# A two-layer equivariant graph network on one core: products in one PSUM tile, node sums turned once and repeated by transfers, layer 1's transfers in fewer shares

## The chip, the cores and the metric

The kernel runs on one core of a Trainium2 chip. The metric is the device time of one execution in microseconds (us), as the median of several executions. The engines are named as in the profile: PE (TensorE, matmuls), PEld (its weight load), DVE (VectorE), ACT (ScalarE), POOL (GpSimd) and SP (SyncE, which here issues transfers).

## The reference

There are N = 6250 nodes with 160 features each (64 scalars, and 32 vectors of 3) and E = 100000 edges, sorted by their target `dst`. Two layers run one after the other, each on the layer-normalised and rectified features, and each is added to `x`.

```
# layer 0
m0, m1 = tp(h[dst], edge_attr_4, wm...)        # one message per edge
msgs   = merge(m0 + lin(h0, lm0), m1 + lin(h1, lm1))
agg    = segment_sum(msgs, src)                # row = src: the messages are NOT sorted by this
a0, a1 = split(agg); x0, x1 = split(h)         # 64 scalars, 32 x 3 vector parts
u0 = einsum('eu,ev,uvw->ew',  x0, a0, wu000) + isq3 * einsum('euk,evk,uvw->ew', x1, a1, wu110)
u1 = einsum('eu,evk,uvw->ewk', x0, a1, wu011) + einsum('euk,ev,uvw->ewk', x1, a0, wu101)
x  = x + h + merge(u0 + lin(x0, lu0), u1 + lin(x1, lu1))
# layer 1
messages = products(h[src], edge_attr_4, W...) * sigmoid(edge_attr_16 @ W_rad.T + b_rad)
agg      = segment_sum(messages, dst)          # sorted by this
x        = x + lin(h + agg, L_s, L_v)
```

The costly part is the product `u`: for each node, two feature vectors `x` and `a` are multiplied in all pairs and the pairs are contracted with weight tensors `wu...`.

## The kernel before

The program has three stages that follow one another.

**scatter()** (L445 to 648) makes layer 0's messages, in 782 tiles of 128 edges. Since they are not sorted by the node that sums them, each tile works out the rank of its edges among those of the same block of nodes (PE L567 and L568), forms the messages on PE (L569), and POOL sends the tile to its places in a DRAM table `msgs` by one indirect transfer (L587). Behind it, the messages of each block of nodes lie together.

**update()** (L650 to 1030) sums the messages per node and forms the product `u`. It goes in 13 groups: twelve of 500 nodes and a last one of 250. For one group:

- `fetch(k)` (L710) loads the messages of four blocks ("a quad") from `msgs` into `urec`, by four transfers that SP issues. Three quads are fetched ahead.
- `sums(g, a)` (L723 to 784) is a generator whose steps are strewn into the group before. `ones` (L728) makes one-hot matrices `uhot` of which message belongs to which node (on ACT, L746 and L749; for group 0 on DVE). PE multiplies them with `urec` (L761, 32 matmuls per quad), which gives the sums with nodes on the partitions. ACT copies them into `ag` (L767, L769), with the 64 scalar columns written twice and each of the three sets of 32 vector columns four times. PE then turns each of the four 128-wide slices (L782), and ACT copies it to `a[:, j]` (L778): `a[:, 0]` is the scalars repeated twice over the 128 partitions, and `a[:, 1..3]` are the vector parts repeated four times.
- `Group.first` (L853) is one of the 32 steps that `plan` lists: 16 of kind "x", 8 of kind "v", 8 of kind "y". Each takes a tile `y` of two PSUM banks from the pool `py`, which has two such tiles. PE fills it by matmuls (L860 for a "y" step, L879 for the others, which merely repeat rows of `x` or `v` over the partitions), and DVE multiplies it with `a` (L882), in a "y" step twice, with `a[:, 1:]` and with `x1k` (L864, two instructions). POOL adds the halves of "y" products (L867), multiplies and adds those of "v" steps (L849, L887).
- `second` (L895) contracts the products with weights on PE into `out0` and `out1`, some steps later (`later`: 2, 8 and 4 steps).
- `back()` (L902 to 974), strewn into the group after, turns the result, adds it to `x`, normalises it and stores what layer 1 gathers, the table `T1` (L972, L973).

The order on PE, DVE, ACT and POOL is written by hand (the loop at L997 to 1025 walks through all steps of all groups); the order of SP's transfers is left to the scheduler. Instructions wait for each other by semaphores, which the framework puts in by following who last read or wrote a tile.

**windows()** (L1059 to 1280) is layer 1, in 131 sets of 6 tiles of 128 edges. POOL gathers the rows of `T1` (L1087, 782 indirect transfers, two sets ahead), PE computes the gates (L1106), ACT and DVE form the messages, and PE adds them into windows of 32 nodes with one-hots `whot` (L1124, L1243). SP writes each window to a DRAM table (L1253), and loads the edge attributes in pieces of `CH` = 2 sets (`piece`, L1042).

A path for other inputs, `general()`, is not run here.

Of the kernel before, what the change touches and what calls it, by code (L numbers as in the profile page):

```python
# [23 lines left out]
P = 128  # L24
# [18 lines left out]
CH = 2  # L43
# [13 lines left out]
def gnn_kernel(ctx: ExitStack, tc: tile.TileContext, a: dict, out: bass.AP):  # L57
# [47 lines left out]
    def edge_attr(pool):  # L105
        t = pool.tile([P, ET, 4], F32, name="attr")
        nc.sync.dma_start(t, a["attr4"])
        return t
# [541 lines left out]
    def update():  # L650
# [3 lines left out]
        with ExitStack() as s:  # L654
# [8 lines left out]
            py = s.enter_context(tc.tile_pool(name="py", bufs=2, space=PSUM))  # L663
# [41 lines left out]
            last = []  # L705
# [4 lines left out]
            def fetch(k):  # L710

                if k >= len(quads):
                    return
                g, q = quads[k]
                b0, nq = groups[g][0] // BW + q, min(4, groups[g][1] // BW - q)
                got[g, q] = recs.tile([P, 4, 4, F + 1], F32, name="urec")
                for b in range(nq):
                    with tc.issue_after(last[-1]) if last else nullcontext():
                        at = nc.sync.value_load(start_i[0:1, b0 + b:b0 + b + 1], min_val=0, max_val=E)
                    last.append(nc.sync.dma_start(got[g, q][:, b], msgs[bass.ds(at, CAP), :]  # L720
                                                  .rearrange("(p i) f -> p i f", i=4)).ins)

            def sums(g, a):  # L723

                r0, n = groups[g]
                qs = [(q, min(4, n // BW - q)) for q in range(0, n // BW, 4)]
                hots, ags = [], []

                def ones(q, nq):


                    rl = two.tile([P, 4, 4], F32, name="rl")
                    nc.scalar.activation(rl[:, :nq], got[g, q][:, :nq, :, F], AF.Copy, scale=-1.0,
                                         bias=float(r0 + q * BW))
                    hot = two.tile([P, 4, 4, 32], F32, name="uhot")
                    hots.append(hot)
                    if g == 0:
                        nc.vector.tensor_tensor(hot[:, :nq].rearrange("p b i n -> p i b n"),
                                                node[:, None, :nq].to_broadcast([P, 4, nq, 32]),
                                                rl[:, :nq].rearrange("p b i -> p i b")[:, :, :, None]  # L740
                                                .to_broadcast([P, 4, nq, 32]), op=OP.add)
                        nc.vector.tensor_single_scalar(hot[:, :nq], hot[:, :nq], 0.0, op=OP.is_equal)
                        return
                    for b in range(nq):
                        for i in range(4):
                            nc.scalar.activation(hot[:, b, i], node[:, b], AF.Square, bias=rl[:, b, i:i + 1])  # L746
                        if b % 2:
                            yield
                    nc.scalar.activation(hot[:, :nq], hot[:, :nq], AF.Relu, scale=-1.0, bias=1.0)  # L749
                    yield  # L750

                yield from ones(*qs[0])
                yield
                for j, (q, nq) in enumerate(qs):
                    if g == 0 and j + 1 < len(qs):
                        yield from ones(*qs[j + 1])
                    p = pt.tile([P, 4 * P], F32, name="ptr")
                    rec, hot = got.pop((g, q)), hots.pop(0)
                    for i in range(4):
                        for b in range(nq):  # L760
                            nc.tensor.matmul(p[32 * b:32 * b + 32, :F], hot[:, b, i], rec[:, b, i, 0:F],  # L761
                                             start=i == 0, stop=i == 3, tile_position=(0, 32 * b))
                    fetch(quads.index((g, q)) + 3)
                    yield
                    w = 32 * nq
                    ag = pool.tile([P, 4, P], F32, name="ag", bufs=5)
                    nc.scalar.copy(ag[:w, 0].rearrange("p (i f) -> p i f", i=2),  # L767
                                   p[:w, None, 0:M0].to_broadcast([w, 2, M0]))
                    nc.scalar.copy(ag[:w, 1:].rearrange("p k (i f) -> p k i f", i=4),  # L769
                                   p[:w, M0:F].rearrange("p (k f) -> p k f", k=3)[:, :, None]  # L770
                                   .to_broadcast([w, 3, 4, M1]))
                    ags.append(ag)
                    if g and j + 1 < len(qs):
                        yield from ones(*qs[j + 1])
                    yield
                for j in range(5):
                    if j:
                        nc.scalar.copy(a[:, j - 1, :n], p[:, :n])  # L778
                    if j < 4:
                        p = pt.tile([P, 4 * P], F32, name="ptr")  # L780
                        for ag, (q, nq) in zip(ags, qs):
                            nc.tensor.matmul(p[:, q * BW:(q + nq) * BW], ag[:32 * nq, j],  # L782
                                             quad[:32 * nq, :nq].rearrange("p b n -> p (b n)"), start=True, stop=True)
                        yield
# [19 lines left out]
            halves = (slice(0, M0), slice(M0, P))  # L804

# [9 lines left out]
            class Group:  # L815
# [37 lines left out]
                def first(self, kind, c):  # L853
# [3 lines left out]
                    y = py.tile([P, 2, 4 * P], F32, name="y")  # L857
# [119 lines left out]
            with tc.manual_schedule(engines={eng.PE, eng.DVE, eng.Activation, eng.Pool}):  # L977
# [13 lines left out]

                for k in range(3):
                    fetch(k)
                gs = {0: Group(0)}
# [39 lines left out]
    def early(pool):  # L1034
# [7 lines left out]
        def piece(k, pool):  # L1042
            t0 = k * CH * GB
            nt = min(CH * GB, ET - t0)
            if nt > 0:
                nq = -(-nt // GB)
                bufs = 3 if pool is e["pool"] else 6
                t = e["attr"][k] = pool.tile([P, CH * GB, 4], F32, name="wattr", bufs=bufs)
                nc.sync.dma_start(t[:, :nt], a["attr4"][:, t0:t0 + nt])
                t = e["blk"][k] = pool.tile([GB * 16 + 1, CH, P], F32, name="wblk", bufs=bufs)  # L1050
                for r in (slice(0, K), slice(K, K + 1)):
                    nc.sync.dma_start(t[r, :nq], a["attr16"][r, k * CH:k * CH + nq])

        e["piece"] = piece
        for k in range(3):
# [3 lines left out]
    def windows(e):  # L1059
# [3 lines left out]
        with ExitStack() as s:  # L1063
# [7 lines left out]
            fin = s.enter_context(tc.tile_pool(name="wf", bufs=3))  # L1071

# [38 lines left out]
            def messages(u, ps):  # L1111
# [12 lines left out]
                nc.vector.tensor_tensor(hot[:, :nt], lane[:, None, :WN].to_broadcast([P, nt, WN]),  # L1124
# [109 lines left out]
            def add(u):  # L1234
                t0, nt = sets[u]
                hot, ms = ready.pop(u)
                for i in range(nt):
# [7 lines left out]
                    if t0 + i == end and (w % 4 == 3 or w + 1 == NW):  # L1245
                        o = pool.tile([P, F], F32, name="wo", bufs=3)
                        nc.scalar.copy(o[:j + WN], state["acc"][:j + WN])  # L1247
                        for x in range(w - w % 4, w + 1):
# [4 lines left out]
                            wrote.append(nc.sync.dma_start(agg[x % 2][bass.ds(row, WN), :],  # L1253
# [4 lines left out]
            with tc.manual_schedule(engines={eng.PE, eng.DVE, eng.Activation, eng.Pool}):  # L1258
                for u in range(2):
                    gather(u)  # L1260
                for k in range(3, 7):
                    e["piece"](k, pre)
# [27 lines left out]
    def parts(const, keep):  # L1290
# [119 lines left out]
        def edges(layer):  # L1410
# [5 lines left out]
            with ExitStack() as s:  # L1416
# [29 lines left out]
                def gate(t0, nt):  # L1446
                    q, half = t0 // GB, t0 % GB // NT
                    k = q // CH
                    if k not in blocks:
                        nq = min(CH, a["attr16"].shape[1] - k * CH)  # L1450
                        blocks[k] = ep.tile([GB * 16 + 1, CH, P], F32, name="blk")
                        nc.sync.dma_start(blocks[k][:, :nq], a["attr16"][:, k * CH:k * CH + nq])
# [264 lines left out]
def _layout(i):  # L1717
# [21 lines left out]

    L0 = {k[7:]: v for k, v in i.items() if k.startswith("L0_gnn_")}  # L1740
# [9 lines left out]
    o["attr4"] = padded(i["edge_attr_4"], nt * P, 0).reshape(nt, P, 4).transpose(1, 0, 2)  # L1750
# [6 lines left out]
    o["attr16"] = t16  # L1757
# [47 lines left out]
```

## Time and profile before

| what | us |
|---|---|
| median of three executions | 3076.58 (3076.5 to 3080.14) |
| the profiled execution | 3756.65 |
| its span in the profile | 3754.5 |
| scatter, from the start to the last scatter's issue | 1367.8 |
| update(), groups 0 to 11, from the first product | 874 |
| update(), last group | about 45 |
| windows() | about 1425 |

The profiled execution took 680 us more than the median. Times within it are compared with each other; a step that is worked out from its rows is put against its own time first. Its mean granted PE clock is 0.744 of full speed: near 1 in `update()`, 0.6 to 0.7 in the two other stages. A row of the profile gives the line of the code, the engine, the operation, the tile written and the tiles read with their partitions and elements, the number of instructions, their busy time and the mean of one in ns, and then the engine's idle time just before them with the instruction that ended it.

### The profile page before, as it was taken

How to read it: one execution, taken by the hardware profiler on the slowest of the kernel's cores; microseconds unless marked ns; L12 is line 12 of the kernel's file. 1: busy time of each engine (PE TensorE's matmuls, PEld its weight loads, DVE VectorE, ACT ScalarE, POOL GpSimd, SP SyncE). 2: the span in 40 equal slices, each digit the busy share in tenths (PEclk: the TensorE clock that was granted, in tenths of full speed). 3: DMA queues.
4: the chain of work that ended last, by engine and by line, in shares of the span. 5: the costliest groups of instructions: out<-in, count | busy, mean ns of one | idle time of the engine just before them, and what ended most of it. 6: DMA issues, size and time to landing. Idle time of an engine off the chain costs nothing.

```text
span 3754.5 us, 47926 instructions
## 1 busy us (share of the span) xinstructions
PE 2422.0 (65%) x12112; PEld 1279.0 (34%) x12112; DVE 2213.9 (59%) x4577; ACT 1546.3 (41%) x5127; POOL 2216.2 (59%) x1864
## 2 busy tenths in 40 slices
PE   5655565655544439999999998455555566655655
PEld 3433344443333323333333332132322233332323
DVE  6564555555544437777877775455655556555554
ACT  4445454554444424544453441333433333333433
POOL 4565565655666637777777775655555555555552
PEclk8677766776766659999999999566766666566666
DMA  6555555654544456665655542445444444445442
GB/s 176 157 167 153 167 162 153 180 162 144 148 126 136 136 173 187 180 183 159 178 178 175 165 119 70 130 131 147 133 136 133 137 139 139 131 135 147 133 132 73
DMA packets 346121, 554.56 MB, mean 148 GB/s; under 512 B 63954, under 2 KB 245168, under 8 KB 339947
## 3 DMA queue, kind: packets, MB, share of 16 engines
q1 hardware_dynamic: 230840, 291.12, 28.3%
q0 software_dynamic: 87584, 218.31, 20.0%
q10 hardware_dynamic: 27411, 41.99, 3.4%
q8 instruction: 99, 1.62, 0.2%
q14 instruction: 187, 1.53, 0.1%
HBM read 418.16 MB, written 133.04 MB: 147 GB/s over the span
## 4 chain that ended last, share of the span: by engine, by line
PE 29%; another core or an unknown queue 21%; DVE 17%; ACT 14%; issue 11%; DMA 4%; SPq 2%; POOL 1%; ACTq 1%; DVEq 0%; POOLq 0%
PE out L895 5%; ACT wm L1118 4%; ACT junk L580 4%; DVE pr L864 4%; PE pmsg L569 3%; PE y L879 2%; PE wbank L1243 2%; PE wgate L1106 2%; PE y L860 2%; PE wbank L1175 2%; DVE wtb L1132 2%; PE rank L568 2%; PE ptr L782 2%; DVE wm L1142 1%
## 5 line engine op out<-in xcount | busy, mean ns | idle before, releaser
L587 POOL DMA_INDIRECT msgs<-rec,pos_i x782 | 780.7, 998 | 572.4 <-issue 216.8
L1087 POOL DMA_INDIRECT wgot<-T,src_i x782 | 739.1, 945 | 635.7 <-issue 427.8
L567 PE MATMUL rank<-seen,every 128*128 128x256 f16 x782 | 264.7, 339 | 500.8 <-ACT junk L580 359.1
L580 ACT ACTIVATE junk<-rank,off 128x256 bf16<-128x256 f32 x782 | 373.2, 477 | 388.1 <-remote 280.4
L569 PE MATMUL pmsg<-tw,d 120*128 120x160 f32 x1564 | 470.5, 392 | 54.1 <-issue 38.7
L1106 PE MATMUL wgate<-wrad,wblk 97*128 97x480 f32 x522 | 376.3, 854 | 175.2 <-issue 127.8
L882 DVE TENSOR_TENSOR pr<-y,a 128x1000 f32<-128x1000 f32 (+1 forms) x312 | 352.4, 1151 | 129.5 <-PE y L879 128.8
L867 POOL TENSOR_TENSOR pr<-pr 128x1500 f32<-128x1500 f32 (+1 forms) x104 | 338.1, 3251 | 148.5 <-DVE pr L864 148.4
L1124 DVE TENSOR_TENSOR whot<-lane,wbank 128x192 f32<-128x192 f32 x131 | 45.8, 349 | 616.1 <-ACT wbank L1232 559.0
L1243 PE MATMUL wbank<-wms,whot 128*32 128x160 f32 x1564 | 255.3, 410 | 217.5 <-ACT wo L1247 102.9
L569 PEld LDWEIGHTS pmsg<-tw,d 120*128 120x128 f32 x1564 | 322.6, 256 | 127.3 <-issue 64.7
L1118 ACT ACTIVATE wm<-wgot,wattr 128x160 f32<-128x160 f32 x782 | 311.1, 398 | 34.8 <-DMA wgot<-T,src_i 11.6
L568 PEld LDWEIGHTS <-upto 128*128 128x128 bf16 x782 | 92.6, 118 | 593.6 <-issue 549.9
L584 DVE CAST pos_i<-pos 128x4 int32<-128x4 f32 x196 | 41.3, 210 | 420.9 <-ACT junk L580 379.5
L1243 PEld LDWEIGHTS wbank<-wms,whot 128*32 128x32 f32 x1564 | 146.4, 144 | 413.1 <-ACT wo L1247 136.6
L1121 ACT ACTIVATE wsg<-wgate 128x480 f32<-128x480 f32 x259 | 137.3, 566 | 351.1 <-remote 180.9
L887 POOL TENSOR_TENSOR ppr<-ppr,pr 128x1000 f32<-128x1000 f32 (+1 forms) x104 | 232.0, 2231 | 75.7 <-DVE pr L882 73.3
L555 DVE TENSOR_TENSOR seen<-seen,hot 128x256 f16<-128x256 f16 x782 | 230.5, 295 | 70.7 <-DVE hot L552 20.0
L568 PE MATMUL rank<-hot,upto 128*128 128x256 bf16 x782 | 267.0, 341 | 5.1 <-remote 3.8
L552 DVE TENSOR_SCALAR hot<-binb,qb 128x256 bf16<-128x256 bf16 x782 | 238.6, 305 | 0.0
L1106 PEld LDWEIGHTS wgate<-wrad,wblk 97*128 97x128 f32 x522 | 128.9, 280 | 311.7 <-issue 227.7
L1142 DVE TENSOR_TENSOR wm<-wm,wtb 128x384 f32<-128x384 f32 (+1 forms) x393 | 221.7, 564 | 13.5
(218 smaller groups left out, 4434.1 us busy)
## 6 DMA issues: line engine op xcount, KB each, us to landing
urec<-msgs SPq DMA_DIRECT2D x250, 322.0 KB
attb<-in_attr SPq DMA_DIRECT2D x48, 960.0 KB
tw<-T0s SPq DMA_DIRECT2D x391, 75.0 KB
xb<-hT SPq DMA_DIRECT2D x192, 125.0 KB
dstb<-in_dstrow SPq DMA_DIRECT2D x48, 480.0 KB
T0s<-tt ACTq DMA_DIRECT2D x11, 1200.0 KB
msgs<-rec,pos_i POOLq DMA_INDIRECT x782
wgot<-T,src_i POOLq DMA_INDIRECT x782
```

Of the source, the lines that this page charges most:

```text
L567: nc.tensor.matmul(rank[:, j % 2], every, before, start=True, stop=False)
L568: nc.tensor.matmul(rank[:, j % 2], upto, hot, start=False, stop=True)
L569: nc.tensor.matmul(prs[-1][:, j % 2, :F], ds[j // WP][:, j % WP], tws[j // WP], start=True, stop=True)
L580: nc.scalar.activation(junk, rank, AF.Relu, bias=off, accum_out=pos[:, j:j + 1])
L587: nc.gpsimd.indirect_dma_start(out=views[(t0 + j) % NV][:, :], out_offset=bass.IndirectOffsetOnAxis(ap=pos_i[:, j:j + 1], axis=0), in_=rec ...
L867: nc.gpsimd.tensor_tensor(prs[0], prs[0], prs[1], op=OP.add)
L882: nc.vector.tensor_tensor(pr[:, :, :n], y[:, :, :n], a[:, j, None, :n].to_broadcast([P, 2, n]), op=OP.mult)
L1087: nc.gpsimd.indirect_dma_start(out=got[u][:, i], out_offset=None, in_=T1[:, :], in_offset=bass.IndirectOffsetOnAxis(ap=src_i[:, t0 + i:t0 ...
L1106: nc.tensor.matmul(p[:, :n], blocks[u // CH][:, u % CH], rad[:, lo * F:lo * F + n], start=True, stop=True)
L1118: nc.scalar.activation(m[:, b, j:j + F], g[:, i, oS1:oS1 + F], AF.Copy, scale=attr(u)[:, i, 0:1])
L1142: nc.vector.tensor_tensor(mv[:, :, :, 0:M0], mv[:, :, :, 0:M0], tb[:, :nt, k].rearrange("p (b t) w -> p b t w", b=h), op=OP.add)
L1243: nc.tensor.matmul(state["acc"][j:j + WN], hot[:, i], ms[:, i], start=t0 + i == w * WT, stop=t0 + i == end, tile_position=(0, j))
```

## The change

- The pool `py` holds one tile `ys` of four banks, made once. A step takes one half of it, `ys[:, turn % 2]`, in turn.
- `ag` holds the sums once (160 columns). PE turns them in two slices, 0 to 128 and 128 to 160. ACT copies the four parts into their place in `a`, and ten transfers from `a` to `a` per group fill the repeats (SP; for group 0 SP and ACT in turn).
- For groups after the first, the one-hots are made two quads ahead instead of one, with three buffers.
- For group 0 the fetches go alternately by SP's and ACT's queue, and the group's other loads are issued before them.
- For layer 1, `attr4` is laid out as 4 × 32 rows and `attr16` as 8 × 12 rows (each with a row of padding, so that the outer dimension stays apart), a piece holds 3 sets (`CH` = 3), and a window's rows are written as 4 × 8, with the one-hots numbered in that order (`order`).

```diff
-CH = 2
+CH = 3
...
-            py = s.enter_context(tc.tile_pool(name="py", bufs=2, space=PSUM))
+            py = s.enter_context(tc.tile_pool(name="py", bufs=1, space=PSUM))
...
-                    with tc.issue_after(last[-1]) if last else nullcontext():
-                        at = nc.sync.value_load(start_i[0:1, b0 + b:b0 + b + 1], min_val=0, max_val=E)
-                    last.append(nc.sync.dma_start(got[g, q][:, b], msgs[bass.ds(at, CAP), :]
-                                                  .rearrange("(p i) f -> p i f", i=4)).ins)
+
+                    o = b % 2 if g == 0 else 0
+                    eng = (nc.sync, nc.scalar)[o]
+                    with tc.issue_after(last[o]) if o in last else nullcontext():
+                        at = eng.value_load(start_i[0:1, b0 + b:b0 + b + 1], min_val=0, max_val=E)
+                    last[o] = eng.dma_start(got[g, q][:, b], msgs[bass.ds(at, CAP), :]
+                                            .rearrange("(p i) f -> p i f", i=4)).ins
...
-                    rl = two.tile([P, 4, 4], F32, name="rl")
+                    rl = two.tile([P, 4, 4], F32, name="rl", bufs=3)
...
-                    hot = two.tile([P, 4, 4, 32], F32, name="uhot")
+                    hot = two.tile([P, 4, 4, 32], F32, name="uhot", bufs=3)
...
-                yield from ones(*qs[0])
+                for q, nq in qs[:1 if g == 0 else 2]:
+                    yield from ones(q, nq)
...
-                    ag = pool.tile([P, 4, P], F32, name="ag", bufs=5)
-                    nc.scalar.copy(ag[:w, 0].rearrange("p (i f) -> p i f", i=2),
-                                   p[:w, None, 0:M0].to_broadcast([w, 2, M0]))
-                    nc.scalar.copy(ag[:w, 1:].rearrange("p k (i f) -> p k i f", i=4),
-                                   p[:w, M0:F].rearrange("p (k f) -> p k f", k=3)[:, :, None]
-                                   .to_broadcast([w, 3, 4, M1]))
+                    ag = pool.tile([P, F], F32, name="ag", bufs=5)
+                    nc.scalar.copy(ag[:w], p[:w, 0:F])
                     ags.append(ag)
-                    if g and j + 1 < len(qs):
-                        yield from ones(*qs[j + 1])
+                    if g and j + 2 < len(qs):
+                        yield from ones(*qs[j + 2])
                     yield
-                for j in range(5):
-                    if j:
-                        nc.scalar.copy(a[:, j - 1, :n], p[:, :n])
-                    if j < 4:
-                        p = pt.tile([P, 4 * P], F32, name="ptr")
-                        for ag, (q, nq) in zip(ags, qs):
-                            nc.tensor.matmul(p[:, q * BW:(q + nq) * BW], ag[:32 * nq, j],
-                                             quad[:32 * nq, :nq].rearrange("p b n -> p (b n)"), start=True, stop=True)
-                        yield
+
+
+                for lo, hi in ((0, P), (P, F)):
+                    p = pt.tile([P, 4 * P], F32, name="ptr")
+                    for ag, (q, nq) in zip(ags, qs):
+                        nc.tensor.matmul(p[:hi - lo, q * BW:(q + nq) * BW], ag[:32 * nq, lo:hi],
+                                         quad[:32 * nq, :nq].rearrange("p b n -> p (b n)"), start=True, stop=True)
+                    yield
+                    for j, at, w in ((0, 0, M0), (1, M0, M1), (2, M0 + M1, M1)) if lo == 0 else ((3, 0, M1),):
+                        nc.scalar.copy(a[at:at + w, j, :n], p[at:at + w, :n])
+                        for to in range(0, P, w):
+                            if to != at:
+                                (nc.scalar if g == 0 and to // w % 2 else nc.sync).dma_start(
+                                    a[to:to + w, j, :n], a[at:at + w, j, :n])
...
+            ys, turn = py.tile([P, 2, 2, 4 * P], F32, name="y"), [0]
...
-                    y = py.tile([P, 2, 4 * P], F32, name="y")
+
+                    y = ys[:, turn[0] % 2]
+                    turn[0] += 1
...
+                gs = {0: Group(0)}
                 for k in range(3):
                     fetch(k)
-                gs = {0: Group(0)}
...
-                bufs = 3 if pool is e["pool"] else 6
+                bufs = 2 if pool is e["pool"] else 4
...
-                nc.sync.dma_start(t[:, :nt], a["attr4"][:, t0:t0 + nt])
+                nc.sync.dma_start(t[:, :nt], a["attr4"][:, :P // 4, t0:t0 + nt])
...
-                for r in (slice(0, K), slice(K, K + 1)):
-                    nc.sync.dma_start(t[r, :nq], a["attr16"][r, k * CH:k * CH + nq])
+                nc.sync.dma_start(t[:K, :nq],
+                                  a["attr16"][:, :K // 8, k * CH:k * CH + nq])
+                nc.sync.dma_start(t[K:, :nq], a["attr16"][0:1, K // 8, k * CH:k * CH + nq])
...
+            order = iota("order", [[1, 4], [4, WN // 4]], 0, 0, pool=pre).rearrange("p a b -> p (a b)")
...
-                    e["piece"](u // CH + 7, pre)
+                    e["piece"](u // CH + 3, pre)
...
-                nc.vector.tensor_tensor(hot[:, :nt], lane[:, None, :WN].to_broadcast([P, nt, WN]),
+                nc.vector.tensor_tensor(hot[:, :nt], order[:, None].to_broadcast([P, nt, WN]),
...
-                            wrote.append(nc.sync.dma_start(agg[x % 2][bass.ds(row, WN), :],
+                            wrote.append(nc.sync.dma_start(agg[x % 2][bass.ds(row, WN), :]
+                                                           .rearrange("(b a) f -> a b f", a=4),
```

In the changed file L860 is L868, L864 is L872, L879 is L887, L882 is L890, L895 is L903, and L761 is L765.

More of the change, by code (lines that the diff above doesn't have):

```diff
@@ L106, in edge_attr @@
         t = pool.tile([P, ET, 4], F32, name="attr")
-        nc.sync.dma_start(t, a["attr4"])
+        nc.sync.dma_start(t, a["attr4"][:, :P // 4])
         return t
@@ L704, in update @@
             nc.gpsimd.memset(eps, EPS)
-            last = []
+            last = {}
             quads = [(g, q) for g, (_, n) in enumerate(groups) for q in range(0, n // BW, 4)]
@@ L1046, in piece @@
                 nq = -(-nt // GB)
-                bufs = 3 if pool is e["pool"] else 6
+                bufs = 2 if pool is e["pool"] else 4
                 t = e["attr"][k] = pool.tile([P, CH * GB, 4], F32, name="wattr", bufs=bufs)
-                nc.sync.dma_start(t[:, :nt], a["attr4"][:, t0:t0 + nt])
+                nc.sync.dma_start(t[:, :nt], a["attr4"][:, :P // 4, t0:t0 + nt])
                 t = e["blk"][k] = pool.tile([GB * 16 + 1, CH, P], F32, name="wblk", bufs=bufs)
-                for r in (slice(0, K), slice(K, K + 1)):
-                    nc.sync.dma_start(t[r, :nq], a["attr16"][r, k * CH:k * CH + nq])
+                nc.sync.dma_start(t[:K, :nq],
+                                  a["attr16"][:, :K // 8, k * CH:k * CH + nq])
+                nc.sync.dma_start(t[K:, :nq], a["attr16"][0:1, K // 8, k * CH:k * CH + nq])
         e["piece"] = piece
-        for k in range(3):
+        for k in range(2):
             piece(k, pool)
@@ L1260, in windows @@
                     gather(u)
-                for k in range(3, 7):
-                    e["piece"](k, pre)
+                e["piece"](2, pre)
                 beside(0)
@@ L1449, in gate @@
                     if k not in blocks:
-                        nq = min(CH, a["attr16"].shape[1] - k * CH)
+                        nq = min(CH, a["attr16"].shape[2] - k * CH)
                         blocks[k] = ep.tile([GB * 16 + 1, CH, P], F32, name="blk")
-                        nc.sync.dma_start(blocks[k][:, :nq], a["attr16"][:, k * CH:k * CH + nq])
+                        K = GB * 16
+                        nc.sync.dma_start(blocks[k][:K, :nq],
+                                          a["attr16"][:, :K // 8, k * CH:k * CH + nq])
+                        nc.sync.dma_start(blocks[k][K:, :nq], a["attr16"][0:1, K // 8, k * CH:k * CH + nq])
                     p = pg.tile([P, NT * F], F32, name="pgate")
@@ L1738, in diagonal, with shares @@
         return np.concatenate(r, 1)
+    def shares(v, k, fill):
+        r = np.full((k, len(v) // k + 1) + v.shape[1:], fill, v.dtype)
+        r[:, :-1] = v.reshape((k, -1) + v.shape[1:])
+        return r
     L0 = {k[7:]: v for k, v in i.items() if k.startswith("L0_gnn_")}
@@ L1749, in _layout @@
     o["attr5"] = np.concatenate([np.ones((1, nt * P), a4.dtype), a4[:, 3:4].T, a4[:, 0:3].T])
-    o["attr4"] = padded(i["edge_attr_4"], nt * P, 0).reshape(nt, P, 4).transpose(1, 0, 2)
+    o["attr4"] = shares(padded(i["edge_attr_4"], nt * P, 0).reshape(nt, P, 4).transpose(1, 0, 2), 4, 0)
     nq = -(-nt // GB)
@@ L1756, in _layout @@
     t16[:-1] = full.reshape(P, nq, GB * 16).transpose(2, 1, 0)
-    o["attr16"] = t16
+    o["attr16"] = shares(t16[:-1], 8, 1)
     o["m0"] = np.concatenate([L0["wm000"][:, 0], L0["lm0"], L0["wm011"][:, 0]], 1)
```

## The prediction

> **What bounds the kernel now.** I read the busy time by stage first, because a share over the whole span mixes three stages (columns: stretch, its length, busy time and instruction count of PE, PEld, DVE, ACT and POOL, granted PE clock, DMA share, GB/s). The last row is one steady group of `update()`.
>
> ```profile
> core 0: us, PE busy (x) PEld busy (x) DVE busy (x) ACT busy (x) POOL busy (x), PEclk, DMA share, GB/s
> 100.00:1365.00 1265.00, 685.75 (x3246) 489.65 (x3244) 666.37 (x2528) 598.20 (x2083) 744.94 (x748) 0.70 0.53 151
> 1411.00:2285.00 874.00, 809.46 (x5253) 298.69 (x5250) 675.40 (x627) 383.39 (x1401) 653.63 (x242) 0.99 0.56 164
> 2330.00:3755.00 1425.00, 814.70 (x2874) 424.09 (x2874) 766.95 (x1097) 507.99 (x1473) 739.14 (x782) 0.63 0.47 132
> 1996.00:2069.00 73.00, 67.97 (x452) 25.52 (x450) 56.68 (x55) 33.45 (x122) 54.77 (x21) 1.00 0.60 175
> ```
>
> In `update()` PE is busy 67.97 of 73.00 us per group (93%), DVE 56.7: PE bounds it, with DVE close behind. In the two other stages no engine is near full; they run at the pace of POOL's 1564 indirect transfers. Where the change acts is therefore told by who waits for whom in `update()` (the waits, 1420 to 2230; total, times, longest):
>
> ```profile
> DVE pr L882 <- PE y L879: 118.5, 78, 4.1
> DVE pr L864 <- PE y L860: 64.0, 79, 2.6
> PE ptr L761 <- ACT uhot L749: 17.5, 10, 1.8
> PE y L879 <- DVE pr L864: 14.5, 22, 1.1
> ```
>
> DVE waits for PE's products `y` (182 us), PE for DVE hardly (14.5). PE can stay ahead because `y` is two deep. The timeline of one "y" step shows it (start, duration, engine, line):
>
> ```profile
> 1912.91 0.58 PE L860 MATMUL y<-x,w_f 64*128 64x500 f32 x1
> 1913.42 1.04 PE L895 MATMUL out<-pr,s 128*32 128x500 f32 x6
> 1913.63 1.72 DVE L864 TENSOR_TENSOR pr<-y,a 128x1500 f32<-128x1500 f32 x1 [0.25 <-PE y L860]
> 1914.39 0.59 PE L879 MATMUL y<-x,pick 96*128 96x500 bf16 x2
> 1914.92 1.06 PE L895 MATMUL out<-pr,w_f 128*64 128x500 f32 x4
> 1915.27 1.71 DVE L864 TENSOR_TENSOR pr<-y,x1k 128x1500 f32<-128x1500 f32 x1
> 1916.90 3.49 DVE L882 TENSOR_TENSOR pr<-y,a 128x1000 f32<-128x1000 f32 x3
> 1917.04 0.59 PE L879 MATMUL y<-v,pickv 96*128 96x500 bf16 x2 [1.06 <-DVE pr L864]
> ```
>
> At 1914.39 PE writes the next step's `y` while DVE works on this one until 1916.98; only the step after that, at 1917.04, waits, for the multiply two steps back (0.06 us after its end).
>
> **The change, part by part.**
>
> *The product tile (dominant).* `py` goes from two tiles of two banks to one tile `ys` of four, whose halves the steps use in turn. In the built program each wait is attached to the tile, not to the half: every step's first `y` matmul waits for the last multiply of the step just before. (Example: the "x" matmul behind a "y" step waits for that step's `x1k` multiply, which reads the other half; in the old program it waited for the multiply before it.) Nothing is saved, and the overlap above is gone: PE's matmul and DVE's multiply alternate. Queued behind the waiting matmul on PE's fixed order are its step's L895, L761, L782, L921, L957 and L967 work; behind DVE, POOL's L867 and L887.
>
> A step then costs the larger of PE's own work and a closed loop. Loop of an x or v step: matmul start to DVE start 0.62 (read at such pairs), multiply 1.17 (row: 1191 ns, pipelined ends overlap a little), hand back 0.06: 1.85. Loop of a y step: four L860 passes 1.06, hand-over 0.12, two multiplies 1913.63 to 1916.98 = 3.35, hand back 0.06: 4.59.
>
> ```profile
> L882 DVE TENSOR_TENSOR pr<-y,a 128x1000 f32<-128x1000 f32 x286 | 334.5, 1191 | 123.7 <-PE y L879 123.0
> L864 DVE TENSOR_TENSOR pr<-y,a 128x1500 f32<-128x1500 f32 x95 | 163.3, 1719 | 68.5 <-PE y L860 68.5
> L864 DVE TENSOR_TENSOR pr<-y,x1k 128x1500 f32<-128x1500 f32 x95 | 162.3, 1709 | 0.0
> L782 PE MATMUL ptr<-quad,ag 128*128 128x100 f32 x456 | 58.6, 281 | 1.5 <-ACT utt L972 1.3
> ```
>
> A group has 8 y and 24 x or v steps: 8 × 4.59 + 24 × 1.85 = 36.7 + 44.4. In seven x/v steps PE's own work (transposes, a quad's sums, turns, T1 products) is longer: 2.44, 1.98, 2.02, 2.59, 4.93, 2.51, 2.53, adding 6.0. Sum 87.1; DVE's small work of `back()` adds about 1: 88 us per group against 73.0, **+15**.
>
> The clock is the second part. With PE working 65.5 of 88 us, three y steps per group have no filler behind their L895 and leave PE idle 2.5 of 4.59 us. The page "TensorE: Matmul & The Clock Gate" of the Trainium skill says (table "Why this matters for your kernels") that an idle window of about 3.4 us brings the half clock, so no gap over some 3 us: by that, 2.5 us gaps cost nothing and the group stays at 88. This trace is stricter. Of its 3.41 us clock windows that were followed by a fall from 1.00 to 0.50 the median was 22% busy and the highest 67%; of those about half busy 11 fell and 13 stayed; and back to 1.00 it took a window at least 83% busy (136 rises). The three gaps put a window near or under half, so I take a fall in most, each with one or two windows at half clock, 2 to 2.5 us: **+6.5**. Both ends: 0 (the page), and the half clock throughout, where 65.5 us of PE work at half rate is about 130 us per group.
>
> *Sums turned once.* The turn L782 is made for two slices, not four: 10 matmuls fewer per group, 10 of 20, and the two runs of 20 take 2.49 and 2.48 us in the timeline, so −2.4 us of PE; one ACT copy 1×160 for two (row of L769: 482 ns for 128x384), −0.4. Added are 10 SBUF-to-SBUF transfers per group on SP (group 0: 6 on ACT, 4 on SP), of 32 or 64 partitions × 2000 B. About 0.4 us of SP issue each (SP's issues in the timeline: 0.47 for one, 1.72 for four) is 4 us, plus 4 us to land (what the T1 stores take). `a` is finished near step 25 of 32 and first read at step 0 of the next group: 7 steps, over 16 us, cover 8. Without that cover: +8 per group. They pass SP's queue behind the T1 stores and x-broadcast loads and before the loads of the group after next, which have a group's time. In the new loop the 2.4 us of PE is mostly hidden, since the loop and not PE sets most steps: I take 0, ends −2.4 and +3.
>
> *One-hots two quads ahead.* Takes away the 17.5 us of L761's wait, 1.75 us per group, which now lies under the loop: 0, ends −1.75 and 0.
>
> *First messages on two queues, loads before fetches.* From the last scatter issue (1367.75) to the first multiply (1411.78) the DMA share is 0.86 at 254 GB/s over 1365 to 1411, so two issuers find engines that are nearly full. Group 0's repeats on SP stand behind group 1's 12 fetches. −1, ends −5 and +5.
>
> *Layer 1.* `attr4` and the agg writes go in 4 shares, `attr16` in 8, pieces hold 18 tiles instead of 12. The page "DMA: Bandwidth & Descriptors" (how many engines) says that the outermost sizes decide how many of the 16 engines carry a transfer, on hardware queues the lowest-numbered: 4 and 8 here. No row shows such a transfer. In 2330 to 3755 SP's queue took 8.4% of 16 × 1425 us for 61579 packets, 31 ns each; a set of 6 tiles has 64 rows of agg, 64 of `attr4`, 48 of `attr16`. Put on 4, 4 and 8 engines instead of 16 this adds some 0.8 us per set to engines 0 to 3, which carry about 5 us of a set whose six gathers take 7.5 (945 ns and 0.30 between). So hidden: 0. If the landing were the limit, 0.8 × 131 = +105; if the smaller spread eases the gathers, −15. The iota `order` costs once.
>
> **Sum.** 12 groups × (88 + 6.5 − 73) = +258; the last half group (x/v multiply 673 ns, y 940 and 929 in its rows) about +6; head −1: **+263 us**. The profiled execution took 3756.65 us around a span of 3754.5; it is 680 longer than the median 3076.58 because of stalls in scatter and windows, none in `update()`. So the step goes over as it is: 3756.65 becomes some 4020, and 3076.6 + 263 = **3340**.
>
> **Rivals.**
> - *Clock kept.* As the page says; +15 × 12 + 5 = +185: 3262. For it: no gap reaches 3.4 us. Against it: the windows of this trace.
> - *Half clock for long stretches.* Recovery needs an almost full window, which the loop seldom gives. 104 to 110 us per group: 3455 to 3530; throughout, 130 us: 3765.
> - *Not serial, faster.* Were each half (or bank) freed by itself on the chip, PE would stay the bound and lose 2.4 (turns), 1.75 (one-hots) and about 0.7 (part of the 14.5 us waits): −4.9 × 12.5 = −61, about 3016. It decides at the first `y` matmul behind a "y" step: does it start with DVE still in `x1k`, or 0.06 us after it? The built program's waits speak against it.
> - *Late repeats.* If the 10 transfers land late at each group's start: up to +8 × 12 = +96 on top, 3436.
> - *Engines 0 to 3 hold up layer 1.* +105 on top: 3445.
>
> **How the numbers follow.** Loop with clock dips 0.55; clock kept 0.20; longer half clock 0.13; late repeats or layer 1 on top 0.05; not serial or the loop's cost outweighed by gains elsewhere 0.05; in balance 0.02. The range 3230 to 3480 holds the first two with their bounds and part of the third. A measurement of this kernel can tell about 0.2%, 6 us. Faster 0.05, same 0.02, slower 0.93.
>
> **What the profile after would show.** Right: in `update()` `y` waits of PE for DVE's `pr` at nearly every step, some hundred us where 14.5 stood; group period 88 to 100; PE busy share near 70 to 75%; clock digits under 9 in that stretch; half the L782 rows; other stages within a few us, group starts with no wait for `a`. Wrong: a `y` matmul that overlaps the preceding step's multiply, PE over 90%, a clock of 0.99, waits of L868 or L890 for the repeats, or gathers spaced wider than before.

## The result, and the profile after

The changed kernel takes 3372.34 us (3368.87 to 3381.38) against 3078.07 us (median of four executions): 1.097 times as long, with a 95% interval of 1.0956 to 1.0988, or 294 us more. Its profiled execution took 3374.04 us, with a span of 3372.2.

On one chip every execution of the kernel before took about 3760 us (3754 to 3775 beside the last experiment), and the profile of before is of that kind: its extra time lies in the scatter and in layer 1 (1367.8 and 1431.9 us, where the changed kernel has 1083.6 and 1033.7), so only `update()` is compared across the two profiles.

Busy time by stage of the changed kernel (columns as before), and in the last row one steady group:

```profile
100.00:1083.00 983.00, 635.77 (x3210) 458.68 (x3208) 673.84 (x2502) 586.18 (x2060) 745.53 (x747) 0.77 0.68 195
1131.00:2300.00 1169.00, 915.34 (x5082) 311.54 (x5081) 702.28 (x645) 355.03 (x1310) 663.35 (x248) 0.88 0.44 129
2340.00:3372.00 1032.00, 721.07 (x2896) 387.72 (x2892) 771.24 (x1106) 502.94 (x1482) 739.50 (x782) 0.73 0.65 183
1270.40:1367.60 97.20, 76.72 (x430) 26.38 (x428) 57.76 (x53) 31.11 (x117) 54.40 (x21) 0.88 0.48 138
```

A group takes 97.2 us in this row, and about 95.5 between most starts of L837 (the first matmul that a group does once), where 73.0 stood before. PE is busy 79% of it, DVE 59%: no engine is full any more. PE's busy time per group is even longer than before (76.7 against 68.0) although it has 2.4 us less to do, while its clock is 0.88 in place of 0.99 to 1.00. The waits of the changed kernel (1230 to 2280) name the loop from both sides; before, PE waited 14.5 us for the multiply and DVE 182.5 for the products:

```profile
DVE pr L890 <- PE y L887: 263.4, 252, 4.2
DVE pr L872 <- PE y L868: 132.9, 79, 3.1
PE y L887 <- DVE pr L872: 109.0, 73, 2.6
PE y L887 <- DVE pr L890: 79.8, 107, 1.7
PE y L868 <- DVE pr L890: 22.4, 60, 0.4
```

The timeline of a y step of the changed kernel, and the two steps after it, shows the loop itself (rows of PE and DVE):

```profile
1295.34 0.58 PE L868 MATMUL y<-x,w_f 64*128 64x500 f32 x1
1295.86 1.04 PE L903 MATMUL out<-pr,s 128*32 128x500 f32 x6
1295.98 1.72 DVE L872 TENSOR_TENSOR pr<-y,a 128x1500 f32<-128x1500 f32 x1 [1.21 <-PE y L868]
1296.83 2.33 PE L781 MATMUL ptr<-quad,ag 128*128 128x100 f32 x20
1297.61 1.71 DVE L872 TENSOR_TENSOR pr<-y,x1k 128x1500 f32<-128x1500 f32 x1
1299.38 0.58 PE L887 MATMUL y<-x,pick 96*128 96x500 bf16 x2 [0.22 <-DVE pr L872]
1299.89 1.06 PE L903 MATMUL out<-pr,w_f 128*64 128x500 f32 x4
1300.00 1.20 DVE L890 TENSOR_TENSOR pr<-y,a 128x1000 f32<-128x1000 f32 x1 [0.67 <-PE y L887]
1301.25 0.58 PE L887 MATMUL y<-v,pickv 96*128 96x500 bf16 x2 [0.30 <-DVE pr L890]
```

The next step's matmul starts at 1299.38, 0.06 us after the `x1k` multiply ended at 1299.32, although it writes the other half of `ys`. The matmul after that starts 0.05 us after the end of the multiply that began at 1300.00. Before, the matmul at the same place started while DVE was in its first multiply.

Three stretches of the trace, from the last scatter's issue to the first product, from there to the last product, and from there to the end, give the account:

| kernel | head | update() | layer 1 |
|---|---|---|---|
| before (profile as above) | 44.0 | 910.8 | 1431.9 |
| changed | 46.1 | 1208.7 | 1033.7 |
| before with one tile (second experiment) | 46.7 | 1314.7 | 1034.3 |

`update()` grew by 298 us, which accounts for the whole loss. Layer 1 with the old transfers takes 1034.3, with the new 1033.7.

### The profile page after: what moved, and what is told of

Read it like the earlier page. It is cut to its first block, busy times and chain, and to the rows that moved or that the text cites. A ratio compares the mean times of both kernels' runs of the same rounds, so it can differ in the third digit from the quotient of the medians.

```text
span 3372.2 us, 47323 instructions
## 1 busy us (share of the span) xinstructions
PE 2388.2 (71%) x11860; PEld 1224.6 (36%) x11860; DVE 2249.8 (67%) x4577; ACT 1510.0 (45%) x5064; POOL 2218.5 (66%) x1865
## 4 chain that ended last, share of the span: by engine, by line
DVE 26%; PE 24%; DMA 19%; POOL 13%; issue 9%; ACT 7%; SPq 1%; ACTq 0%; DVEq 0%; POOLq 0%
DMA msgs<-rec,pos_i 11%; POOL wgot L1099 10%; DVE pr L872 9%; DVE pr L890 6%; PE y L887 5%; PE out L903 5%; DMA wgot<-T,src_i 4%; POOL msgs L587 4%; PE y L868 4%; ACT junk L580 2%; ACT wm L1130 2%; DVE wtb L1144 2%; DVE wm L1154 2%; PE pmsg L569 2%; PE wbank L1187 1%
## 5 line engine op out<-in xcount | busy, mean ns | idle before, releaser
L1099 POOL DMA_INDIRECT wgot<-T,src_i x782 | 739.5, 946 | 257.3 <-issue 210.5
L569 PE MATMUL pmsg<-tw,d 120*128 120x160 f32 x1564 | 451.8, 378 | 187.1 <-ACT rec L582 186.6
L890 DVE TENSOR_TENSOR pr<-y,a 128x1000 f32<-128x1000 f32 (+1 forms) x312 | 361.6, 1159 | 305.8 <-PE y L887 305.8
L569 PEld LDWEIGHTS pmsg<-tw,d 120*128 120x128 f32 x1564 | 306.6, 244 | 258.9 <-ACT rec L582 232.0
L1255 PE MATMUL wbank<-wms,whot 128*32 128x160 f32 x1564 | 234.2, 384 | 182.0 <-DVE wms L1157 106.9
L1118 PE MATMUL wgate<-wrad,wblk 97*128 97x480 f32 x522 | 336.3, 781 | 22.8 <-ACT wsg L1133 14.0
L895 POOL TENSOR_TENSOR ppr<-ppr,pr 128x1000 f32<-128x1000 f32 (+1 forms) x104 | 231.1, 2222 | 148.7 <-DVE pr L890 128.8
L872 DVE TENSOR_TENSOR pr<-y,a 128x1500 f32<-128x1500 f32 (+1 forms) x104 | 172.7, 1661 | 184.9 <-PE y L868 156.1
L887 PE MATMUL y<-x,pick 96*128 96x500 bf16 (+1 forms) x416 | 130.8, 399 | 217.5 <-DVE pr L872 138.4
L582 ACT COPY rec<-pmsg 128x320 f32<-128x320 f32 x391 | 163.5, 418 | 213.2 <-DMA msgs<-rec,pos_i 203.9
L568 PE MATMUL rank<-hot,upto 128*128 128x256 bf16 x782 | 253.5, 324 | 3.8 <-DVE hot L552 3.7
L903 PE MATMUL out<-pr,w_f 128*64 128x500 f32 (+1 forms) x832 | 250.3, 685 | 0.0
L749 ACT ACTIVATE uhot<-node,rl 128x32 f32<-128x32 f32 x920 | 201.4, 307 | 1.9
```

Of the source, the lines that this page charges most:

```text
L569: nc.tensor.matmul(prs[-1][:, j % 2, :F], ds[j // WP][:, j % WP], tws[j // WP], start=True, stop=True)
L872: nc.vector.tensor_tensor(pr[:, :, :n], y[:, i, None, :n].to_broadcast([P, 3, n]), other, op=OP.mult)
L887: nc.tensor.matmul(y[:, i, :n], w.rearrange("p i v -> p (i v)"), rhs, start=True, stop=True)
L890: nc.vector.tensor_tensor(pr[:, :, :n], y[:, :, :n], a[:, j, None, :n].to_broadcast([P, 2, n]), op=OP.mult)
L903: nc.tensor.matmul(out[part, :self.n], w, pr[:, i, :self.n], start=k in self.fresh, stop=self.left[k] == 0)
L1099: nc.gpsimd.indirect_dma_start(out=got[u][:, i], out_offset=None, in_=T1[:, :], in_offset=bass.IndirectOffsetOnAxis(ap=src_i[:, t0 + i:t0 ...
```

## Experiments

They are told in the order in which they ran. Each ratio is against the kernel before on the same chip (3074.72 us for experiments 1 to 4, 3070.07 for 5 to 8). The 32 steps of a group are counted from 0. A step's time is worked out from the trace: from the start of its first multiply to that of the next step, as a mean over groups 2 to 10 (the first group is 0). In the diffs, `...` marks lines left out.

**1. Two tiles in turn again, the rest of the change kept.**

```diff
-            py = s.enter_context(tc.tile_pool(name="py", bufs=1, space=PSUM))
+            py = s.enter_context(tc.tile_pool(name="py", bufs=2, space=PSUM))
...
-            ys, turn = py.tile([P, 2, 2, 4 * P], F32, name="y"), [0]
...
-                    y = ys[:, turn[0] % 2]
-                    turn[0] += 1
+                    y = py.tile([P, 2, 4 * P], F32, name="y")
```

> The changed kernel with only the product tile put back: two tiles of two banks in turn, as before; everything else of the change stays. Theory (the wait on the whole tile makes the loss): the group period falls from 95.5 back to 73 or a little less, and since two turns and the one-hot wait (2.4 and 1.75 us per group) are gone and PE bounds again, the time is 3020 to 3070. Rival (the repeat transfers, the loads behind them or layer 1's fewer shares have a good part in the loss): 3100 or more.

Measured: 3080.15 us, 1.0017 of before (1.0005 to 1.0028); `update()` 911.8 us. The tile explains the loss, since putting it back removes it. But the other parts, which were expected to give 5 to 60 us, gave nothing. The waits of this kernel (1200 to 1990) show where part of that went:

```profile
DVE uxo L931 <- DMA uxo<-xs: 22.3, 11, 5.3
PE ptr L927 <- DVE uxo L931: 10.4, 8, 4.0
```

The timeline of this kernel explains it (start, and time in which the transfers were issued on SP's queue; then DVE's row):

```profile
1553.28 6.84 SPq L788 DMA_DIRECT2D a<-a  x10
...
1577.68 1.35 SPq L307 DMA_DIRECT2D uxo<-xs  x2
...
1582.39 0.32 DVE L931 TENSOR_TENSOR uxo<-uxo,ptr 128x160 f32<-128x160 f32 x1 [3.08 <-DMA uxo<-xs]
```

Ten repeats take SP 6.84 us to issue, not the 4 that the prediction took. `a` is in time, but the load of `uxo`, behind them in SP's queue, is late: DVE waits in its fixed order for it (2.0 us per group, once 5.3), and its next multiply with it. The step where that happens, step 5, grew from 2.09 to 3.31 us.

**2. The kernel before with only the one tile.**

```diff
-            py = s.enter_context(tc.tile_pool(name="py", bufs=2, space=PSUM))
+            py = s.enter_context(tc.tile_pool(name="py", bufs=1, space=PSUM))
...
+            ys, turn = py.tile([P, 2, 2, 4 * P], F32, name="y"), [0]
...
-                    y = py.tile([P, 2, 4 * P], F32, name="y")
+                    y = ys[:, turn[0] % 2]
+                    turn[0] += 1
```

> The kernel before with only the product tile changed to one tile of four banks whose halves are used in turn. Theory: the loop of PE and DVE appears alone, group period 94 to 97, total 3340 to 3375. Rival (other parts make most of the loss): under 3200.

Measured: 3479.97 us, 1.1303 (1.1261 to 1.1345). The tile alone costs 405 us, more than the whole change; the expectation missed by over 100, because it took the places of the other PE work from the changed kernel. In the old order a quad's sums (L761) stand in the x step behind a y step (steps 5, 9, 13, 17 and 21). The timeline of this kernel (some rows of PE and DVE):

```profile
1764.36 1.04 PE L897 MATMUL out<-pr,s 128*32 128x500 f32 x6
1766.12 1.71 DVE L866 TENSOR_TENSOR pr<-y,x1k 128x1500 f32<-128x1500 f32 x1
1767.88 0.58 PE L881 MATMUL y<-x,pick 96*128 96x500 bf16 x2 [2.48 <-DVE pr L866]
1768.39 1.93 PE L897 MATMUL out<-pr,w_f 128*64 128x500 f32 x4
1770.25 2.02 PE L761 MATMUL ptr<-urec,uhot 128*32 128x160 f32 x32
```

PE stands 2.48 us in the y step with nothing to do, and then has the sums in a step where DVE waits. Behind the gap the clock is at half (a clock record of 0.50 for 3.41 us starts at 1768.3): the same L897 group that takes 1.06 at full clock takes 1.93, and the sums take 2.02 in place of 1.30.

**3. A filler that keeps PE busier.** In the changed kernel, each contraction of a y product is followed by one with zero weights.

```diff
+            none = wp.tile([P, M1], F32, name="none")
+            nc.gpsimd.memset(none, 0.0)
...
+                        if o == 1:
+                            assert k not in self.fresh
+                            nc.tensor.matmul(out[part, :self.n], none, pr[:, i, :self.n], start=False,
+                                             stop=self.left[k] == 0)
```

> The changed kernel with PE kept busier in the y steps: behind each of the three contractions of a y product there is one more matmul of the same size, with weights of zero (adds nothing to the sums; about 1.0 us more PE work per y step, 8 us per group, in a gap of 2.5 us). Theory (about 7 us of each group's 95.5 are half clock that the gaps bring): fewer falls of the clock, group period 88 to 91, total 3280 to 3320. Rival A (the loop alone is 95 us long, the clock has no part in it): no gain, 3370. Rival B (PE's own work decides more steps than thought): +4 to +8 per group, 3420 to 3470.

Measured: 3329.9 us, 1.0818 (1.0777 to 1.0859); 42 us less than the changed kernel, although PE has about 7 us more to do per group (a y product's contractions take 1.89 us with the filler and 1.04 without). By the trace's clock records, the half clock between the first product and the last half group fell from 274 to 113 us (278 and 117 in the expectation of experiment 7; the fall is the same). So the clock has a part; the gain is less than expected, in part because the filler lengthened y steps that already held sums or turns (20 by 0.4, 24 by 0.6 us), and 113 us of half clock were left.

**4. One tile for each bank.** In the changed kernel, four tiles of one bank; the x and v multiplies are split in two.

```diff
-            py = s.enter_context(tc.tile_pool(name="py", bufs=1, space=PSUM))
+            py = s.enter_context(tc.tile_pool(name="py", bufs=4, space=PSUM))
...
-                    y = ys[:, turn[0] % 2]
-                    turn[0] += 1
+                    y = [py.tile([P, 4 * P], F32, name="y") for _ in range(2)]
...
-                    nc.vector.tensor_tensor(pr[:, :, :n], y[:, :, :n], a[:, j, None, :n].to_broadcast([P, 2, n]),
-                                            op=OP.mult)
+                    for i in range(2):
+                        nc.vector.tensor_tensor(pr[:, i, :n], y[i][:, :n], a[:, j, :n], op=OP.mult)
```

> The changed kernel with the products in four tiles of one bank each, taken in turn, two per step; the multiply of an x or v step becomes two instructions of 128x500 (673 ns each in the old profile's last group, so about 0.15 us more of DVE per step, 3.6 per group). This is a tile per bank, so a bank is waited for by itself. Theory (waits follow tiles): PE runs ahead again, DVE at some 62 us stays under PE, group period 69 to 73, total within 20 us of the version with two tiles. Rival (DVE's extra instructions lengthen its part until it bounds): period 75 to 80, 3100 to 3150.

Measured: 3087.03 us, 1.0033 (1.0021 to 1.0044); `update()` 917.3. The same four banks, told apart by tiles, lose 7 us against two tiles and not 294, so it is not the banks that make PE and DVE take turns. Finer release than two tiles of two banks brings nothing either, which fits the little that PE waited for DVE there. The two halves cost DVE 669 ns each:

```profile
L889 DVE TENSOR_TENSOR pr<-y,a 128x500 f32<-128x500 f32 x575 | 352.8, 669 | 81.0 <-PE y L885 80.9
```

**5. The repeats by ACT.** Experiment 1 with the ten repeats issued by ACT.

```diff
-                                (nc.scalar if g == 0 and to // w % 2 else nc.sync).dma_start(
+                                (nc.scalar if g or to // w % 2 else nc.sync).dma_start(
```

> Product tiles in turn again (as in the first experiment), and the ten repeat transfers of every group issued by ACT, right behind ACT's own copies, instead of SP. In the first experiment DVE waited 22.3 us in 11 groups for the load of uxo, which SP issued behind the repeats, and PE for DVE then. Theory (the repeats on SP ate the gain of the fewer turns and the earlier one-hots): the wait goes, the group period falls by about 2 us to 70.5, total 3045 to 3060 against 3080. Rival (ACT's ten issues, about 0.5 us each, hold up its copies for PE): 3075 to 3100.

Measured: 3068.19 us, 0.9983 (0.997 to 0.9997). The wait goes as expected:

```profile
DVE uxo L931 <- DMA uxo<-xs: 3.7, 1, 3.7
```

Step 5 falls from 3.31 to 1.33 us, and `update()` from 911.8 to 901.7. The rest of the expected gain did not come: step 16 grew from 3.56 to 4.05, and steps 19, 21 and 24 stayed above before's.

**6. The changed kernel with the one-hots one quad ahead again.**

```diff
-                for q, nq in qs[:1 if g == 0 else 2]:
-                    yield from ones(q, nq)
+                yield from ones(*qs[0])
...
-                    if g and j + 2 < len(qs):
-                        yield from ones(*qs[j + 2])
+                    if g and j + 1 < len(qs):
+                        yield from ones(*qs[j + 1])
```

> The changed kernel with only the one-hots put back to one quad ahead. One tile alone made the old kernel 3480, the whole change 3372; the steps behind a y step (5, 9, 13, 17, 21, 25 of 32) were 0.9 to 2.8 us longer each there. Theory (the earlier one-hots move the sums of the quads from these x steps into the y steps, where the loop leaves PE 2.5 us free): the sums go back, about 5 us per group, total 3415 to 3450. Rival (the two turns saved are what made the difference, and the one-hots nothing): 3370 to 3385.

Measured: 3422.74 us, 1.1133 (1.1105 to 1.1161), 50 us more than the changed kernel. In the loop, the one-hots' place decides that of the sums: four of the five quads' sums move from the y steps 8, 12, 16 and 20 to the steps 5, 9, 13 and 17 (the fifth stays in 21). Steps 5, 9, 13 and 17 grew from 3.55, 2.26, 1.87 and 1.98 to 4.98, 3.40, 3.80 and 3.21 us (7 and 11 fell by 1.9 and 0.8). In the changed kernel such sums lie in the y step, beside DVE's two multiplies (some rows of PE and DVE):

```profile
1282.05 0.62 PE L903 MATMUL out<-pr,s 128*32 128x500 f32 x3
1282.17 1.72 DVE L872 TENSOR_TENSOR pr<-y,a 128x1500 f32<-128x1500 f32 x1 [1.84 <-PE y L868]
1282.91 1.27 PE L765 MATMUL ptr<-urec,uhot 128*32 128x160 f32 x30
1283.80 1.71 DVE L872 TENSOR_TENSOR pr<-y,x1k 128x1500 f32<-128x1500 f32 x1
1285.57 0.58 PE L887 MATMUL y<-x,pick 96*128 96x500 bf16 x2 [0.32 <-DVE pr L872]
```

The other 57 us between this kernel and experiment 2 stand beside the two turns saved; steps 17, 21 and 25 are 1.2, 1.1 and 1.9 us shorter, and the turns of experiment 2 fill steps 24 and 25 where here they fill 24 alone.

**7. Two fillers instead of one.** As 3, with the zero-weight matmul twice.

> As the third experiment, with two matmuls with zero weights behind each contraction of a y product instead of one, some 2 us in the gap of 2.5. With one, the half clock fell from 278 to 117 us over the stage and the stage by 51.5 us, 0.32 us for each us of half clock. Theory (the clock is the rest of the loss beside the loop): the half clock falls to under 60 us, the stage by 20 more, total 3300 to 3320. Rival (the filler now is longer than the gap wherever a quad's sums lie in it too): 3330 to 3380.

Measured: 3481.25 us, 1.1326 (1.1307 to 1.1345). The rival holds, and further than it said: the half clock did fall to 77 us, but y steps 8, 12, 16, 20 and 24 now take 6.14 to 7.15 us in place of 4.02 to 4.81. The second copy costs more than the first: a y product's contractions take 4.44 us, so the two copies add 3.4 us and not 2. With a quad's sums behind them, PE's work runs past the multiplies (step 12 of one group; L874, L889, L905 and L767 are the changed kernel's L872, L887, L903 and L765, and L911 is the filler; some rows of PE and DVE):

```profile
1692.80 1.02 PE L905 MATMUL out<-pr,s 128*32 128x500 f32 x2
1694.55 1.71 DVE L874 TENSOR_TENSOR pr<-y,x1k 128x1500 f32<-128x1500 f32 x1
1696.65 0.58 PE L911 MATMUL out<-pr,none 128*32 128x500 f32 x1
1697.07 1.25 PE L767 MATMUL ptr<-urec,uhot 128*32 128x160 f32 x22
1698.26 0.59 PE L889 MATMUL y<-x,pick 96*128 96x500 bf16 x2
```

DVE's second multiply ends at 1696.26, but the next step's matmul starts only at 1698.26, when the sums are through. Why the second copy costs three times the first stays open.

**8. Experiment 5 with the one-hots one quad ahead again.** The edit of 6 on the kernel of 5.

> The first kernel of this call with the one-hots one quad ahead again. Theory (with PE ahead of DVE it matters little in which step the sums lie; only the wait for the one-hots, 1.6 us per group, comes back): 15 to 25 us above the first kernel of this call. Rival (the sums behind the y step's contractions cost as much as the wait saved): within 5 us of it, or faster.

Measured: 3050.48 us, 0.993 (0.9912 to 0.9948), `update()` 882.2 us. The theory said 15 to 25 us more, and it is 18 less. What helps in the loop hurts when PE is ahead: with the sums out of steps 8, 12, 16 and 20 again, steps 16, 19, 20, 21 and 24 fall by 0.8, 1.0, 0.2, 0.8 and 1.3 us, while 17 and 5 grow by 1.4 and 0.4. Part of it is seen in the waits: in experiment 5 PE's turn waited for ACT's `utt` copies, 11.7 us in 9 groups, and 0.5 us here. The rest could not be put to one wait, and stays open. This version is faster than both kernels.

**9. The filler only in the four gaps that have room.** Against the changed kernel:

```diff
                         return [(prs[0], 1, [(slice(M1 * k, M1 * k + M1), s1[:, 28 - 4 * c:][:, :M1])
-                                             for k in range(3)])]
+                                             for k in range(3)], c in (0, 2, 6, 7))]
...
+                        if gap:
+                            assert k not in self.fresh
+                            nc.tensor.matmul(out[part, :self.n], none, pr[:, i, :self.n], start=False,
+                                             stop=self.left[k] == 0)
```

The y items 0, 2, 6 and 7 are contracted in steps 4, 12, 28 and 0.

> As the third experiment (one matmul with zero weights behind each contraction of a y product), but only in the four y steps of a group whose PE work has room for it (0, 4, 12 and 28 of 32: they kept 4.02 to 4.11 us with the filler of the third experiment, while 8, 20 and 24, where a quad's sums or turns lie, grew by 0.4 to 0.7). Theory (in these gaps the clock falls; the loop alone is 86 to 89 us of the 95.5): half clock falls at least as far as with the filler everywhere (117 us over the stage) or not much less, no y step gets longer, total 3300 to 3335. Rival (the falls come from other places too, so filling four gaps leaves most of them): half clock over 200 us, 3345 to 3370.

Measured: 3997.78 us against 3763.07 for before on the same chip, 1.061 (1.0577 to 1.0643): 235 us more, where the whole change gave 294. The absolute times that were expected don't apply on this chip; the stage does, and its undisturbed steps take the same 1.87, 1.94, 2.41 and 4.02 us as in the changed kernel. All of `update()` in this kernel:

```profile
1425.00:2557.30 1132.30, 902.17 (x5554) 317.89 (x5556) 723.66 (x676) 362.56 (x1332) 683.21 (x260) 0.96 0.46 135
```

and in the changed kernel:

```profile
1129.70:2338.40 1208.70, 947.96 (x5242) 323.95 (x5241) 723.62 (x676) 362.49 (x1332) 681.97 (x260) 0.87 0.43 126
```

The stage is 76 us shorter with more PE instructions in it; the clock is 0.96 in place of 0.87, PE's busy time falls by 46 us, and the half clock between the first product and the last half group is 74 us in place of 274. No y step is longer than before the filler. The theory holds: gaps of 2.5 us bring the clock down, and the falls then lengthen the steps behind them (step 5 is 2.23 us here and 3.55 without the filler, step 7 2.66 and 4.51). The rival has a smaller part: 16 of 41 falls remain, 12 of them in steps 10 and 26, which got no filler.

## Why the prediction was right

The prediction was 3340 with a range of 3230 to 3480; 3372 came out, 294 us more than before where the sum had 263. The 31 us that the sum lacks lie in the twelve groups (277 from first to last start of L837, in place of 258) and in the last half group (18 in place of 6). Point by point:

- *The tile.* Right. Each step waits for the one just before, at 0.05 to 0.06 us, and putting the two tiles back (experiment 1) takes the loss away. The rival "each half freed by itself" is excluded by the same rows, and experiment 4 shows that the banks are not the cause.
- *The loop.* Right. In the changed kernel the steps with nothing else in their way take 4.02 us (y), 2.41 (the one before a y step) and 1.87 to 1.94 (the others). That is 8 × 4.02 + 8 × 2.41 + 16 × 1.9 = 81.8 us per group, where the sum had 36.7 + 44.4 = 81.1. For the whole loop the sum had 88. Between the changed kernel and experiment 9 the twelve groups went from 1148.1 to 1075.4 us while the half clock went from 274 to 74: 0.36 us for each us of half clock. Carried on to no half clock, this gives 100 us in 12 groups, 8.3 per group, and leaves 87.4 for the loop. That last step is an extrapolation; 6.1 us per group were in fact taken away.
- *The clock.* Right in mechanism and near in size: 6.5 us per group was taken and 6.1 to 8.3 found. The clock fell 41 times in twelve groups, 27 of them in steps 0, 4 and 28, the three steps of a group with a PE gap over 2 us. A fall lasted 6.3 us in the mean, and at 0.36 that costs 2.3 us, where 2 to 2.5 was taken. By the rule of the page "TensorE: Matmul & The Clock Gate" of the Trainium skill (table "Why this matters for your kernels"), which asks only for no idle gap over some 3 us, there would have been no fall, since from group 1 on no PE gap was over 2.57 us. The measurement decides here. Cut into the 3.41 us windows of its clock records, the changed kernel repeats what the trace of before had shown: of its windows at full clock in these twelve groups all 27 in which PE was under 45% busy were followed by a fall, 14 of 20 from 45 to 55%, and none of 210 above. What the sum did not follow up is that PE's own work runs longer at half clock: its share came to 79%, over the 70 to 75 that were named.
- *The last half group.* Mis-sized: +6, and it was +18 (from its L837 to the last product 37.6 before, 55.8 after). Why is not shown; the 45 us set down for it before took in some 8 us behind the last product.
- *Turns, one-hots, repeats: 0.* Right as the sum was made, which names one quad's sums among its seven longer x and v steps, as the changed kernel has it (step 21). As a statement about the parts it hides two large terms. On top of one tile, they are worth 108 us (3480 to 3372), 50 of them by the one-hots alone, which put the sums into the y steps' gaps.
- *The repeats' cover.* The cover named was the time until `a` is read, and that held: DVE waited for a transfer into `a` once, before the first product. With PE ahead, what was not priced is who stands behind them in SP's queue: `uxo`'s load, 2 us per group (experiments 1 and 5). The issue took 0.58 us each in the median, 0.68 in the row above, not 0.4.
- *The rival at 3016.* Its price was wrong. With PE ahead, all other parts came to +5 us, not -61. Of these 66 us the late `uxo` load took 10 (experiment 5) and the new places of the sums 18 (experiment 8); the other 38 were not traced.
- *Head and layer 1: -1 and 0.* Right: the head 46.1 against 46.7 and layer 1 1033.7 against 1034.3, compared with experiment 2, which has the old code for both. In the head it came out as the prediction put it, the repeats behind the fetches on SP. The first turn starts at 1114.98 in the changed kernel and at 1120.06 in experiment 2, and ACT's share of the repeats is issued by 1123.3, but SP's four come after 16 fetches, and the first multiply waits for one of them (timeline of the changed kernel):

```profile
1101.55 23.57 SPq L723 DMA_DIRECT2D urec<-msgs  x16
...
1125.22 2.54 SPq L788 DMA_DIRECT2D a<-a  x4
...
1129.77 1.72 DVE L872 TENSOR_TENSOR pr<-y,a 128x1500 f32<-128x1500 f32 x1 [17.19 <-DMA a<-a]
```


## What to carry to other kernels

A ring of two tiles and one tile with two halves use the same memory, but not the same waits: look in the built program at what the second producer waits for before a ring is merged. When a producer and a consumer alternate, place the producer's other work in the steps where the consumer is long; when the producer is ahead, the same place can cost (the one-hots gave 50 us in one case and took 18 in the other). A transfer that is hidden itself still delays what its queue issues next.

## What the runs showed of the hardware

- Gaps of 2.5 us on PE, three in a group of 95 us, went with a clock of 0.87; a fall lasted from 3.41 up to 13.65 us in the clock records, and filling four gaps with about 0.85 us of useless matmuls each saved 76 us.
- Falls followed the busy share of a 3.41 us window: in the changed kernel's twelve groups 27 of 27 windows under 45% were followed by one, 14 of 20 from 45 to 55%, and 0 of 210 above. Experiment 9 had 16 falls left, though hardly a gap from group 1 on was over 1.71 us (one of 2.48).
- One zero-weight matmul behind each contraction made a y product's contractions 1.89 us long in place of 1.04, two made them 4.44.
- Layer 1's transfers in 4 and 8 shares in place of the old ones changed the stage by under 1 us; POOL is busy with its 782 gathers for 739.5 of some 1032 us. Which engines carried the transfers, no run here shows.
